# Group-norm statistics moved to ScalarE, and six of eight bases of the last image taken from a neighbour, in a four-layer convolution network

## The chip, the cores and the metric

One NeuronCore of a Trainium2 chip runs the whole batch. The metric is the device time of one launch in microseconds; before the change it is 15807.8 us, the median of three runs from 15794.6 to 15817.1.

A core has TensorE (PE, matmuls into PSUM), VectorE (DVE), ScalarE (ACT, activation functions), GpSimd (POOL, almost unused here) and SyncE (SP), whose queue issues all DMAs. Each engine works through its own instructions in order; semaphores order them across engines.

## The reference, cut to what matters

The input is 8 images of 32 channels, 256 x 256, in fp32. Four layers follow, each `x = x + layer(group_norm(x))`, with 16 groups of two channels:

```python
def _gn(v, G=16, eps=1e-5):          # mean and variance over 2 channels x 256 x 256
    g = v.reshape(B_, G, C_ // G, H_, W_)
    return ((g - mean(g)) / sqrt(var(g) + eps)).reshape(v.shape)

x = x + conv_dynamic(_gn(x))         # layer 0: a 5x5 depthwise filter pooled from the image
x = x + adder(_gn(x))                # layer 1: out[f] = -sum |patch - w[f]| over 32 x 3 x 3, 8 bit
x = x + conv3x3(_gn(x))              # layer 2
x = x + kan_block(_gn(x))            # layer 3
```

Layer 3 has four small KAN networks on 8 x 8 windows. Each normalises its input over 16 or 32 values, takes eight Gaussian bases of every value, and multiplies bases and a SiLU of the input by weights:

```python
GRID = jnp.linspace(-2.0, 2.0, 8); DENOM = 4.0 / 7.0
basis = jnp.exp(-((ln[..., None] - GRID) / DENOM) ** 2)
out = basis.reshape(..., -1) @ ws.T + jax.nn.silu(x) @ wb.T + bb
```

## The kernel before

A chunk is a tile of 128 partitions (four bands of 32 channels) by 2048 fp32 values, eight rows of each band; an image has eight chunks. The layers are the functions `stage0` to `stage3`.

**The planner.** Nothing is issued as it is written down. `Plan.add` records tasks: an engine, an expected time, a rank, the buffers read and written. `Plan.run` then walks through time with these expected times and writes down one order of tasks for all engines: whenever an engine is free it takes the ready task of lowest rank whose buffers fit. That order is what is compiled; on the chip it is fixed. Ranks are in images: layer 1 of image `b` runs beside layers 2 and 3 of image `b-1` and layer 0 of later images. The last image's layers 2 and 3 have no layer 1 beside them; this stretch is called the tail here.

**Buffers.** `ROOM` (line 68) gives places of fixed kinds: three `bas` for bases, three `si`, two `rs`, one `xr`, and a common arena `sb` of ten chunks; `NDV` gives three `dv` slots, used by layer 1 only. In PSUM there is one four-bank place `psB` for layers 0, 2 and 3, one two-bank place `psA` for layer 1 (and for halves of a chunk in the last image's layer 3, `parts`, line 1219), and two one-bank places `psV`.

**Layer 1** is the filler. A pass (`Pass`) makes a quarter of the channels of a quarter of an image: 72 distances `max(q - w, 0)` (line 996 on DVE, whole; line 998 on ACT, in halves, where ACT has been idle), each followed by eight matmuls that add it into `psA` (line 1018). Sixteen passes make an image. PE takes a waiting distance whenever two are queued (`URGENT`), otherwise its other work. At a pass's end ACT evicts `psA` into `xr` (line 1065), the gate of the next pass.

**Statistics.** Every group norm reads its chunks by `add_stats` (line 637): four `bn_stats` of 512 on DVE for a chunk. They follow the eviction that made the chunk, or for layer 0 the load. `finish` (line 647) joins them by `bn_aggr`, averages over partitions by two small matmuls and takes the reciprocal root by hand on DVE. Layer 0 also takes row sums of five overlapping column ranges (`pool`, line 746). Layer 1's input is scaled on ACT (line 967), clipped and rounded by two DVE instructions (972, 973). Layer 2's chunks are normalised on DVE (line 1131).

**Layer 3** goes chunk by chunk (a unit). For each of the four networks: centre by matmul and evict (1234), square (1239), variance by matmul into `psV` (1247), Ln and Exp for the root (1260, 1264), spread by matmul (1279), multiply on DVE (1287). Then `kan`: eight bases, each a Square with bias (1384) and an Exp in place (1397) on ACT. When layer 1 is wholly done, the planner may give the first of the two to DVE instead (`square.other`):

```python
nc.vector.scalar_tensor_tensor(sb(bas), sb(rb), kb2[:, n, k : k + 1], sb(rb), ALU.add, ALU.mult)
```

(line 1390), with the Exp's bias making up for the constant. Eight groups of 16 matmuls in the program (32 in the trace, as fp32) add the bases into `psB` (line 612), then the SiLU part; ACT evicts (1462). The first of the eight waits in the planner until a few bases are done (`HOLD`).

## Time and profile before

| | |
|---|---|
| median of three runs | 15807.8 us |
| profiled execution, its own time | 15810.7 us |
| its span, first to last instruction | 15808.7 us |
| DVE / PE / ACT busy over the span | 85% / 81% / 78% |
| granted TensorE clock, mean | 0.921 |
| first distance on DVE | 435.4 us |
| last distance on DVE | 14485.6 us |

The eight images' layer 1, cut where each image's last `psA` eviction ends, takes 1443, 1942, 1883, 1907, 1737, 1713, 1713 and 1718 us; 1320 us follow. In the first of these stretches no layer 3 runs yet; in the second to fourth, layer 0 of the later images runs beside it; it is all done early in the fifth. A busy PE is not a PE at its peak, since the ends of matmuls are modelled, and a group's mean may hold several shapes.

### The profile page before, as it was taken

The numbers are of one execution on the slowest core, as the hardware profiler recorded it, in microseconds if no ns is written. First come the engines' busy times: TensorE is split into PE (matmuls) and PEld (weight loads), VectorE is DVE, ScalarE is ACT, GpSimd is POOL, SyncE is SP. The second block draws the span as 40 slices with busy tenths as digits, with TensorE's granted clock in tenths as the row PEclk, the third lists the DMA queues.
The fourth block names the chain that finished last, engine by engine and source line by source line (L and its number), as shares of the span: only waits on it lengthen the run. The fifth ranks groups of instructions, "written<-read, shape, count | busy, mean of one in ns | idle before, by whom it ended". The sixth has DMA issues, their size and how long they took to land.

```text
span 15808.7 us, 560681 instructions
## 1 busy us (share of the span) xinstructions
PE 12814.9 (81%) x260296; PEld 4330.4 (27%) x260296; DVE 13427.1 (85%) x12536; ACT 12262.5 (78%) x6849; POOL 33.1 (0%) x25
## 2 busy tenths in 40 slices
PE   6889897887897888888887888778878887887666
PEld 4223232322222222223222222222222222222222
DVE  2898989789878889888899999999999989997465
ACT  0888848678648778676778997799879987997687
POOL 0000000000000000000000000000000000000000
PEclk9989898998998999999999999999999999998777
DMA  4342345446435444554545554454544454444554
GB/s 117 74 101 55 99 118 160 108 123 169 98 97 157 130 118 125 140 139 105 133 123 142 140 131 126 114 140 123 130 127 130 127 128 129 130 132 112 148 154 134
DMA packets 1192870, 1970.85 MB, mean 125 GB/s; under 512 B 362752, under 2 KB 878848, under 8 KB 1092224
## 3 DMA queue, kind: packets, MB, share of 16 engines
q1 hardware_dynamic: 1190528, 1934.98, 46.6%
q8 instruction: 2036, 33.36, 0.9%
q14 instruction: 306, 2.51, 0.1%
HBM read 1162.83 MB, written 771.75 MB: 122 GB/s over the span
## 4 chain that ended last, share of the span: by engine, by line
PE 22%; ACT 20%; DVE 6%; issue 6%; DMA 1%; SPq 0%; DVEq 0%; ACTq 0%
PE psB L612 9%; PE psA L1018 7%; ACT bas L1384 5%; ACT bas L1397 4%; DVE dv L996 3%; ACT arena L1384 2%; PE psB L1148 2%; ACT arena L1397 2%; ACT arena L1234 2%; PE psB L892 1%; ACT si L1462 1%; ACT arena L1239 1%; DVE arena L1287 1%; PE psV L1247 1%; DVE arena L1390 1%
## 5 line engine op out<-in xcount | busy, mean ns | idle before, releaser
L996 DVE TENSOR_SCALAR dv<-qh,w1q 128x4128 bf16<-128x4128 bf16 (+1 forms) x8815 | 10491.2, 1248 | 1358.8 <-PE psA L1018 1289.9
L1018 PE MATMUL psA<-dv,sel_b 128*32 128x512 bf16 x71048 | 5420.4, 403 | 1421.8 <-DVE dv L996 1155.5
L1018 PEld LDWEIGHTS <-sel_b 128*32 128x32 bf16 x82944 | 2047.6, 97 | 6763.7 <-issue 5758.6
L1384 ACT ACTIVATE bas<-arena,kb 128x2048 f32<-128x2048 f32 x1396 | 2782.5, 1993 | 411.8 <-DVE arena L1287 258.6
L1397 ACT ACTIVATE bas<-bas 128x2048 f32<-128x2048 f32 x1396 | 2671.6, 1914 | 40.1
L998 ACT ACTIVATE dv<-qh,w1n 128x2064 bf16<-128x2064 bf16 x832 | 1635.9, 2009 | 1157.6 <-PE psA L1018 1042.0
L612 PE MATMUL psB<-bas,tl 32*32 32x512 f32 x48544 | 1953.2, 653 | 438.8 <-ACT bas L1397 240.1
L892 PE MATMUL psB<-arena,wt 32*32 32x512 f32 (+1 forms) x51040 | 1848.8, 606 | 122.2 <-issue 69.4
L612 PE MATMUL psB<-arena,tl 32*32 32x512 f32 x22368 | 918.8, 619 | 104.0 <-ACT arena L1397 29.0
L612 PEld LDWEIGHTS psB<-bas,tl 32*32 32x32 f32 x48544 | 526.5, 107 | 1327.5 <-ACT bas L1397 514.2
L892 PEld LDWEIGHTS psB<-arena,wt 32*32 32x32 f32 x51040 | 657.5, 104 | 814.0 <-issue 611.4
L1384 ACT ACTIVATE arena<-arena,kb 128x2048 f32<-128x2048 f32 x407 | 810.0, 1990 | 0.0
L1397 ACT ACTIVATE arena<-arena 128x2048 f32<-128x2048 f32 x407 | 779.1, 1914 | 11.6
L643 DVE BATCH_NORM_STATS2 tiny<-arena 128x6 f32<-128x512 f32 x768 | 473.7, 680 | 345.4 <-ACT arena L925 246.4
L1018 PE MATMUL psA<-qh,sel_b 128*32 128x512 bf16 x9216 | 666.3, 394 | 92.1 <-DMA qh<-q 76.8
L1287 DVE TENSOR_TENSOR arena<-psB,arena 128x2048 f32<-128x2048 f32 x280 | 640.0, 2286 | 59.0 <-PE psB L1279 55.9
L1462 ACT ACTIVATE si<-psB,cols_sb 128x2048 f32<-128x2048 f32 x192 | 377.0, 1963 | 385.0 <-PE psB L612 331.5
L612 PE MATMUL psB<-si,tl 32*32 32x512 f32 x14080 | 618.8, 624 | 32.4 <-DVE arena L1287 13.8
L1148 PE MATMUL psB<-arena,tl 32*32 32x510 f32 (+3 forms) x16384 | 626.6, 610 | 19.9 <-issue 19.8
L1239 ACT ACTIVATE arena<-arena 128x2048 f32<-128x2048 f32 x320 | 612.4, 1914 | 9.8
L925 ACT ACTIVATE arena<-psB,cc 128x2048 f32<-128x2048 f32 x64 | 125.6, 1962 | 536.0 <-PE psB L913 536.0
L1234 ACT ACTIVATE arena<-psB 128x2048 f32<-128x2048 f32 x224 | 418.9, 1870 | 127.1 <-PE psB L612 126.5
(151 smaller groups left out, 7406.4 us busy)
## 6 DMA issues: line engine op xcount, KB each, us to landing
arena<-x SPq DMA_DIRECT2D x128, 1024.0 KB
arena<-y SPq DMA_DIRECT2D x128, 1024.0 KB
si<-sy SPq DMA_DIRECT2D x512, 256.0 KB
arena<-in_x_dram SPq DMA_DIRECT2D x240, 384.0 KB
arena<-in_x_dram SPq DMA_DIRECT2D x256, 256.0 KB
x<-arena SPq DMA_DIRECT2D x256, 256.0 KB
xr<-x SPq DMA_DIRECT2D x512, 128.0 KB
x<-xr SPq DMA_DIRECT2D x512, 128.0 KB
```

What stands on the lines that cost most here:

```text
L612: nc.tensor.matmul(view(o[j * C : (j + 1) * C, i - first, :]), w_, src(rows, i, j), start=start, stop=stop)
L892: nc.tensor.matmul(o[:, lo - 2 * j : hi - 2 * j, c0:c1], wt[rows, t, :], d[rows, lo + dy + 2 : hi + dy + 2, c0 + dx : c1 + dx], start=firs ...
L996: nc.vector.tensor_scalar(dst, src, w1q[:, at : at + 1], 0.0, ALU.subtract, ALU.max)
L998: nc.scalar.activation(dst, src, AF.Relu, bias=w1n[:, at : at + 1])
L1018: nc.tensor.matmul(psA[j * C : (j + 1) * C, i, :], sel_b[:, n, :], src[:, at : at + 2, t % 3 : t % 3 + W], **flags,)
L1148: nc.tensor.matmul(o[:, lo - 2 * j : hi - 2 * j, c0:c1], (wc if t == 4 else tl[:, W2T + t, :])[rows], d[rows, lo + dy + 1 : hi + dy + 1, c ...
L1234: lambda ps=ps, at=at: nc.scalar.activation(sb(c)[:, at], ps().rearrange("p s f -> p (s f)"), func, bias=shift),
L1239: plan.add("ACT", 1.9, lambda: nc.scalar.activation(sb(sq), sb(c), AF.Square), r=[c], w=[sq], rank=rk)
L1287: lambda ps=ps, at=at: nc.vector.tensor_tensor(sb(c)[:, at], ps().rearrange("p s f -> p (s f)"), sb(c)[:, at], ALU.mult),
L1384: lambda k=k, bas=bas: nc.scalar.activation(sb(bas), sb(rb), AF.Square, bias=kb[:, n, k : k + 1]),
L1397: lambda k=k, bas=bas, square=square: nc.scalar.activation(sb(bas), sb(bas), AF.Exp, scale=-1.0, bias=0.0 if square.eng == "ACT" else kbsq ...
L1462: nc.scalar.activation(sb(o), psB.rearrange("p s f -> p (s f)"), AF.Identity, bias=obias)
```

## The change

1. **Statistics.** Sums come from the accumulator output of the evictions that made the chunks (layer 0: from the row sums, less the columns counted twice). Squares come from a Square on ACT with an accumulator, shifted by the first chunk's mean (`add_squares`), in place of `bn_stats`. The squares themselves go to a scratch half behind the chunk, so that chunks and `xr` are longer.
2. **Layer 2's normalisation** goes from DVE to ACT.
3. **The clip** of layer 1's input comes after the rounding, on bf16.
4. **Last image, layer 3.** Of eight bases, numbers 2 and 5 are made by Square and Exp, both on ACT. The other six are a neighbour times `exp(2v)` or `exp(-2v)` times a constant, one `scalar_tensor_tensor` on DVE each; the two ratios are two Exp on ACT of a clamped input (one DVE instruction).
5. **Choice of engine.** When layer 1 is wholly done, the planner may also give the evictions and squares of the variances to DVE (`evict.other`, `square.other`). The product of line 1390 stays for images before the last.
6. **Buffers.** In the same stretch bases and `si` may take the `dv` slots. `BASE_SPARE` goes from three chunks to two, `HOLD` from 4 to 3. In the last image two `si` loads of the third network may start after the first base, not the fifth. A rule on PE's order (`AHEAD`) goes.

```diff
-ROOM = [("bas", 3 * BASE, BASE), ("si", 3 * F, F), ("rs", F // 2, F // 4), ("xr", F // 2, F // 2), ("sb", 10 * F, 0)]
-AHEAD = 9.0
+CHAIN = ((2, None), (5, None), (3, 2), (1, 2), (4, 5), (6, 5), (0, 1), (7, 6))
+MID, FAR = 3, 20.0
+ROOM = [("bas", 3 * BASE, BASE), ("si", 3 * F, F), ("rs", F // 2, F // 4), ("xr", 3 * F // 4, 3 * F // 4), ("sb", 10 * F, 0)]
-BASE_SPARE = 3 * F
-HOLD = 4
+BASE_SPARE = 2 * F
+HOLD = 3
...
             if b.base:
-                b.kind = "bas" if self.places["bas"] else "sb"
+                b.kind = "bas" if self.places["bas"] else "dv" if self.over() and self.places["dv"] else "sb"
                 spare = BASE_SPARE
+            if b.side:
+                b.kind = "si" if self.places["si"] or not self.over() else "dv" if self.places["dv"] else "sb"
...
-                        if best is not None and e == "PE" and best.rank > self.image() + AHEAD:
-                            piece = self.fill(e, False)
-                            if piece is not None:
-                                best = piece
...
+    def over(self):
+        return all(p.done for p in self.passes[self.first_pass :])
...
+        def add_squares(self, src, at, i, size, rank):
+            if not self.chunks & 1 << i:
+                self.chunks |= 1 << i
+                plan.add(
+                    "DVE", 0.16,
+                    lambda: nc.vector.tensor_scalar(
+                        self.shift[:, i : i + 1], self.sums[:, at : at + 1], -1.0 / size, None, ALU.mult
+                    ),
+                    r=[src, self.summed], w=[self.shifted[i]], rank=rank,
+                )
+            plan.add(
+                "ACT", 0.25 + 0.85e-3 * size,
+                lambda: nc.scalar.activation(
+                    sb(src)[:, size : size + size // 2].bitcast(BF16), sb(src, size), AF.Square, bias=self.shift[:, i : i + 1],
+                    accum_out=self.squares[:, at : at + 1],
+                ),
+                r=[src, self.shifted[i]], w=[self.bufs[at]], rank=rank,
+            )
...
+                total, both = norm.sums[:, k : k + 1], norm.d[:, 0, 0:1]
+                nc.vector.tensor_reduce(total, rowsum[:, :, k * R : (k + 1) * R], AX.XY, ALU.add)
+                nc.vector.tensor_reduce(both, v[:, :, 51:205:51], AX.XY, ALU.add)
+                nc.vector.tensor_tensor(total, total, both, ALU.subtract)
-            norm.add_stats(xt, 4 * k, [], r(0.02 * k))
-            plan.add("DVE", 2.9, pool, r=[xt], w=[rs_buf[k]], rank=r(0.02 * k))
+            plan.add("DVE", 3.4, pool, r=[xt], w=[rs_buf[k], norm.summed], rank=r(0.02 * k))
+            norm.add_squares(xt, k, 0, F, r(0.02 * k))
...
-            norm1.add_stats(xt, 4 * k, [], rk)
+            norm1.add_squares(xt, k, 0, F, rk)
...
-                    nc.vector.tensor_scalar(sb(t, F), sb(t, F), QMAX, -QMAX, ALU.min, ALU.max)
                     nc.vector.tensor_scalar(q16(t), sb(t, F), ROUND, ROUND, ALU.add, ALU.subtract)
+                    nc.vector.tensor_scalar(q16(t), q16(t), QMAX, -QMAX, ALU.min, ALU.max)
...
-                norm.add_stats(xr, 8 * g + 2 * h, [], rk, 2)
+                norm.add_squares(xr, NH * g + h, g, F // 2, rk)
...
-                nc.vector.tensor_scalar(sb(xt), sb(xt), norm.mean, norm.rs, ALU.subtract, ALU.mult)
-            plan.add("DVE", 1.7, normal, r=[norm.done], w=[xt], rank=rk)
+                nc.scalar.activation(sb(xt, 10 * W), sb(xt, 10 * W), AF.Identity, bias=nmr, scale=norm.rs)
+            plan.add("ACT", 2.4, normal, r=[sm["c2"]], w=[xt], rank=rk)
...
-            norm3.add_stats(xo, 4 * k, [], rk)
+            norm3.add_squares(xo, k, 0, F, rk)
...
+                evict.other = "DVE", 0.15 + 2.1 * us, lambda ps=ps, at=at: nc.vector.tensor_scalar(
+                    sb(c)[:, at], ps().rearrange("p s f -> p (s f)"), shift, None, ALU.add
+                )
...
+            square.other = "DVE", 2.3, lambda: nc.vector.tensor_tensor(sb(sq), sb(c), sb(c), ALU.mult)
...
+            if last:
+                up, down = Buf("sb", F), Buf("sb", F)
+                plan.add(
+                    "DVE", 1.3,
+                    lambda: nc.vector.tensor_scalar(sb(up), sb(rb), kmax[:, n : n + 1], kmin[:, n : n + 1], ALU.min, ALU.max),
+                    r=[rb], w=[up], rank=rk, spare=SPARE,
+                )
+                for o, sign, bias in ((down, -2.0, kdn[:, n : n + 1]), (up, 2.0, kb2[:, n, MID : MID + 1])):
+                    plan.add(
+                        "ACT", 1.9,
+                        lambda o=o, sign=sign, bias=bias: nc.scalar.activation(
+                            sb(o), sb(up), AF.Exp, scale=sign, bias=bias
+                        ),
+                        r=[up], w=[o], rank=rk, table=LN_EXP, spare=SPARE,
+                    )
+            for k, k0 in chain:
+                bas = bases[k]
+                if k0 is not None:
+                    ratio = up if k > k0 else down
+                    by = float(np.exp(2 * (MID - k0) * (k - k0) - 1))
+                    exps.append(plan.add(
+                        "DVE", 2.4,
+                        lambda bas=bas, k0=k0, ratio=ratio, by=by: nc.vector.scalar_tensor_tensor(
+                            sb(bas), sb(bases[k0]), by, sb(ratio), ALU.mult, ALU.mult
+                        ),
+                        r=[bases[k0], ratio], w=[bas], rank=rk,
+                    ))
+                    continue
...
-                square.other = "DVE", 2.45, product
+                square.other = None if last else ("DVE", 2.45, product)
```

The evictions of layers 0, 1 and 2 also gain `accum_out=` a column of `sums`. The ranks of layer 3's parts are written out by the caller (`beside`) and, but for the SiLU of `z`, are the same numbers.

## The prediction

> **What bounds the kernel now.** I read the page's shares and slices first, then the busy time of stretches cut where an image's sixteenth `psA` eviction (L1065) ends, then the waits inside them, then groups by form. The page:
>
> ```profile
> PE 12814.9 (81%) x260296; PEld 4330.4 (27%) x260296; DVE 13427.1 (85%) x12536; ACT 12262.5 (78%) x6849; POOL 33.1 (0%) x25
> ...
> PEclk9989898998998999999999999999999999998777
> ```
>
> No engine is saturated, and the last slices are another regime. By stretch (an image with a chunk of layer 0 beside it, one without, then the two parts of the tail):
>
> ```profile
> 3818.00:5701.00 1883.00, 1601.41 (x33804) 513.97 (x33800) 1627.29 (x1549) 1320.41 (x730) 6.21 (x2) 0.94 0.47 122
> ...
> 11058.00:12771.00 1713.00, 1393.02 (x26884) 448.70 (x26884) 1583.16 (x1343) 1486.22 (x836) 3.90 (x2) 0.94 0.49 129
> ...
> 14489.00:14710.00 221.00, 146.94 (x3412) 75.03 (x3412) 87.34 (x119) 81.87 (x46) 0.00 (x0) 0.79 0.53 136
> 14710.00:15809.00 1099.00, 718.91 (x12840) 235.97 (x12832) 634.99 (x323) 860.53 (x532) 0.00 (x0) 0.74 0.53 146
> ```
>
> Columns: length, then busy PE, PEld, DVE, ACT, POOL, clock, DMA share, GB/s. Without layer 0, DVE is busy 1583 of 1713 us (92%), ACT 87%. With it, PE rises to 85%, DVE falls to 86% and ACT to 70%. The tail, last image alone, has ACT at 78%, PE at 65%. Waits of the layer-0 stretch:
>
> ```profile
> PE psA L1018 <- DVE dv L996: 105.5, 182, 5.0
> ...
> DVE dv L996 <- PE psA L1018: 223.3, 235, 20.4
> ```
>
> There DVE waits on PE twice as long as PE on DVE. In 11058 to 12771 it is the reverse: PE on DVE 190, DVE on PE 114. So the main part is bound by both, coupled through three `dv` slots. The rows that price the change:
>
> ```profile
> L643 DVE BATCH_NORM_STATS2 tiny<-arena 128x6 f32<-128x512 f32 x768 | 473.7, 680 | 345.4 <-ACT arena L925 246.4 <-ACT arena L1164 73.1 <-DMA arena<-in_x_dram 21.5
> ...
> L1390 DVE SCALAR_TENSOR_TENSOR arena<-arena,kb 128x2048 f32<-128x2048 f32 x124 | 285.5, 2346 | 4.2 <-PE psV L1247 3.3 <-issue 0.9
> ...
> L967 ACT ACTIVATE arena<-arena,cc 128x2048 f32<-128x2048 f32 x64 | 132.8, 2087 | 28.8 <-DMA arena<-x 28.8
> ...
> L1131 DVE TENSOR_SCALAR arena<-arena,tiny 128x2560 f32<-128x2560 f32 x64 | 102.8, 1608 | 25.1 <-DMA arena<-x 25.1
> ```
>
> **What the Trainium skill says.** "ScalarE: Activation LUTs", What ACT_TABLE_LOAD costs: any function costs 0.833 ns per element, 280 ns fixed with a pointer bias, 93 ns more per pointer. That gives 1990 at 2048 (L1384: 1993) and 2.5 us for the new 2560-wide normalisation (L967, two pointers: 2087 at 2048). "VectorE: DVE Perf Modes", the perf-mode tier table: fp32 tensor_scalar 1227 ns at 2048 (L973: 1227), bf16 693. The same page, Two Vector instructions with no wait between them, calls an accumulator output two instructions; whether ScalarE's is, and its time, no row here shows.
>
> **The change, in the trace's sum.** Profiled execution: span 15808.7, its own time 15810.7, median 15807.8; these are one number. Counts by image come from the order of the built programs, durations from the rows, counted start to start where an engine runs back to back (four bn_stats take 2.39 us, a distance 1.23, an L1390 2.29).
>
> *DVE in the main part.* 1024 bn_stats go; 84 of them stand before DVE's first distance and 34 in the tail, so 906 x 0.60 = 544 us. Normalisation moves to ACT: 56 x 1.55 = 87. The clip runs on bf16: 56 x 0.55 = 31. Added: three small sums per layer-0 chunk (some 0.45 us, about 25), and 83 full distances that ACT did in halves (83 x 1.23 less 27 halves of 0.70 = 83). Statistics' small operations cancel against bn_aggr. Fourteen scalings (2.25) and some other stage-3 work go to the tail, about 36. With what moves across the boundaries the orders give, image by image, 1308, 1679, 1629, 1652, 1619, 1587, 1600, 1585 before (within 2% of the measured busy times) and 1204, 1592, 1568, 1533, 1560, 1552, 1559, 1537 after: 12659 to 12105, 554 less.
>
> *ACT in the main part.* Added: 168 squares of 2048 (1.95) and 127 of 1024 (1.1), 468 us; 56 normalisations of 2.5, 140. Accumulator reads, some 560: nothing at the low end, 0.28 us (one short pointer instruction) at the high; I take 0.2, 112. Gone: 139 distance halves x 2.0, 278; and the stage-3 work of the last image but one that the new order leaves for the tail: 95 bases (3.9 us a pair), 12 evictions and their squares, some 450. Sum: about level (11285 to 11255), by image 1250, 1375, 1401, 1360, 1429, 1409, 1558, 1473. ACT has room except in image 6 (1558 against 1486).
>
> *PE.* No matmul is dropped. Three units of stage 3 (about 55 us each at 1.08 per block of 32) leave the main part, and layer 0 spreads: 8 chunks an image to image 5, where the old order had 11 to 14 in images 1 to 3. At 0.49 us per gather and 1.06 to 1.10 per block, images 0 to 7 go from 1144, 1473, 1445, 1460, 1270, 1244, 1245, 1250 to 1068, 1369, 1361, 1349, 1385, 1377, 1255, 1255.
>
> *What that is worth.* The eight stretches of before (1443 to 1942 us) are fitted within 12 us by 0.74 PE + 0.68 DVE - 292, and images 1 to 7 within 9 by 0.80 PE + 0.45 DVE. The weights say what a microsecond off DVE buys while the engines wait on one another. On the new work they give 460 and 340 off the main part. ACT at its best share so far (0.877) would hold image 6 near 1776 us where they want 1700, so I take 370.
>
> *Start-up.* The first eight chunks are paced by DVE (bn_stats 2.4 + pooling 2.45). With statistics on ACT the DMA sets it: 10 saved. The layer-0 taps that follow are PE's; nothing else moves.
>
> *Tail.* It now begins with 117 bases of the last image but one (22 before): 3.7 units of stage 3 mixed with layer 2. Up to the last layer-2 eviction ACT goes from 80 to 396 us of work, DVE from 88 to 313, PE from 113 to 286. At 0.80 on ACT that is 495 us instead of 221: 274 more. Behind it, eight units of the last image alone. A group of eight bases cost up to eight products (2.3) on DVE and eight exponentials on ACT; now two squares, two ratios and two exponentials on ACT (6 x 1.95) and one clamp and six products on DVE (1.25 + 13.8). With 45 halves of evictions and 20 squares moved to DVE: ACT 849 to 603, DVE 637 to 694, PE unchanged. ACT was 77% busy over 1099 us. If DVE takes that share, 694/0.77 = 900: 200 less. Each product waits for its neighbour's exponential and for both ratios; behind it on DVE stand the next group's scalings, and behind those PE's broadcasts, which already wait 92 us there for L1287. Six bas and dv places instead of three (dv lies idle in the tail), and lower HOLD and spare, I cost at nothing: they let the bases run ahead of the single `psB`, which is what makes the 77% possible; without that cover PE would wait as it does now for L1397 (51.6 + 27.9), some 80 us. Net of the tail: 75 longer.
>
> Queues: SP issues 6280 DMAs in both, and each xt or xr is now released by a square instead of bn_stats; the residual load behind it has most of a 107 us pass to arrive. The shift that a square waits for is one tiny DVE instruction, once per group. Evictions now have a square behind them on ACT, about 2 us before the next exponential: paid above.
>
> Sum: -10 - 370 + 75 = -305, so **15500 us**, 1.9% less.
>
> **Rivals.** *DVE is the bound throughout.* For: 92% in images 5 to 7. Main shrinks by 554/0.894 = 620 and the tail stays level, since three engines now share it: 15180. Against: DVE's waits on PE with layer 0.
> *PE is the bound.* For: the waits of 3818 to 5701, and matmul work is untouched. Only 117 of PE work leaves the main part: 117/0.83 = 140 less, tail 75 more, start 10 less: 15730.
> *The debt comes due in the tail (slower).* The mechanism is the backlog of 117 bases, run where there is no distance work to fill gaps. If its part goes at 0.65 on ACT (610) and the units behind at 0.66 on DVE (1050), as coupled groups on one `psB` and a clock of 0.74 would have it, the tail grows by 340; with PE bounding the main part (150 less) the kernel ends at 16000. It decides once the tail outgrows what is saved ahead of it: beyond 1700 us (now 1320) against the forecast's 380, beyond 1480 against 160.
>
> **How the numbers follow.** A measurement tells 0.2% (30 us) from nothing. Forecast 0.58, DVE-bound 0.18, PE-bound 0.14, debt 0.10. The forecast's own range, fit of 340 to 460 and tail of -20 to +160, is 15320 to 15620. Reaching to the two faster cases' middles: 15200 to 15740, leaving the debt and the ends. Faster: everything but the debt and a sliver of the PE case, 0.87; same 0.04; slower 0.09.
>
> **What would show it.** Right: last distance ends at 14080 to 14150; images 1 to 5 even at 1760 to 1820, 6 and 7 at 1680 to 1780; DVE's share in the main part still 88 to 91%; no bn_stats rows; squares at 1.95 to 2.0; the tail near 1400, layer 2 ending near 500 into it, then units of 105 to 120 us. Wrong: ACT above 90% in images 4 to 7 (accumulators dearer than 0.3 us), or PE's waits on DVE gone while DVE's on PE grow (PE-bound), or units at 130 us again.

## The result and the profile after

The changed kernel takes 15624.0 us (median of four, 15616.6 to 15634.7) against 15808.5 for the kernel before in the same comparison: a ratio of 0.9885, 95% interval 0.9868 to 0.9902. The forecast was 15500. The profiled execution has a span of 15620.1, 188.6 less than before. Cut as the prediction cut it, that is 8 from the start-up, 533 from the eight stretches of the main part (1231, 1800, 1790, 1734, 1784, 1763, 1750, 1671 us for images 0 to 7), and 353 back in the tail.

The page of the changed kernel, the two rows shown of before:

```profile
PE 12724.2 (81%) x260296; PEld 4307.3 (28%) x260296; DVE 13070.3 (84%) x12057; ACT 12264.1 (79%) x7416; POOL 21.2 (0%) x25
...
PEclk9989999999999999999999999999999999987677
```

The shares hardly moved. DVE lost 357 us in all, ACT gained 2, and the low clock of the tail now covers the last four slices where it covered three. The busy time of stretches, cut at the same events (length, then busy PE, PEld, DVE, ACT, POOL, clock, DMA share, GB/s): image 2 with layer 0 beside it, image 7 without, and the two parts of the tail.

```profile
3456.00:5246.00 1790.00, 1502.66 (x30906) 484.65 (x30898) 1554.85 (x1476) 1396.30 (x852) 2.69 (x2) 0.95 0.49 128
...
12277.00:13948.00 1671.00, 1365.74 (x26116) 433.80 (x26108) 1526.68 (x1281) 1473.11 (x878) 1.37 (x1) 0.94 0.48 129
13948.00:14530.00 582.00, 360.90 (x8094) 162.98 (x8094) 301.09 (x166) 400.18 (x240) 0.00 (x0) 0.74 0.53 137
14530.00:15621.00 1091.00, 701.85 (x12870) 263.23 (x12870) 695.26 (x417) 606.43 (x379) 0.00 (x0) 0.72 0.55 149
```

The main part ends at 13948 instead of 14489. The first part of the tail (last layer-1 eviction to last layer-2 eviction) grows from 221 to 582 us. The second (the eight units of the last image) takes 1091 where it took 1099, although ACT has 254 us less to do in it. The waits of the layer-0 stretch, on PE and then on DVE (us in total, how many, the longest):

```profile
PE psA L1073 <- DVE dv L1051: 134.0, 239, 2.8
...
DVE dv L1051 <- PE psA L1073: 210.1, 218, 31.7
```

Before, over 1883 us, they were 105.5 and 223.3. DVE still waits longer on PE than PE on DVE, but the gap is narrower. The rows by form that answer to the priced ones (count, then busy us and mean ns of one; bn_stats is gone):

```profile
L675 ACT ACTIVATE arena<-arena,tiny 128x2048 bf16<-128x2048 f32 x192 | 383.6, 1998 | 67.8 <-DMA arena<-in_x_dram 42.0 <-DVE tiny L668 23.0
L1467 DVE SCALAR_TENSOR_TENSOR bas<-bas,arena 128x2048 f32<-128x2048 f32 x81 | 185.0, 2290 | 80.2 <-ACT bas L1488 44.9 <-PE psB L623 34.7
L1188 ACT ACTIVATE arena<-arena,cc,tiny 128x2560 f32<-128x2560 f32 x64 | 159.8, 2511 | 0.0
...
L1028 DVE TENSOR_SCALAR arena<-arena 128x2048 bf16<-128x2048 bf16 x64 | 44.4, 694 | 2.2
L1448 DVE TENSOR_SCALAR arena<-arena,kmax,kmin 128x2048 f32<-128x2048 f32 x32 | 43.1, 1347 | 1.3
...
L675 ACT ACTIVATION_READ_ACCUMULATOR arena<-arena,tiny 128x1 f32 x192 | 36.0, 187 | 0.0
```

The large prices of the prediction hold: squares 2.0 us, the normalisation 2.51 (2.5), a product 2.29 (2.3), the bf16 clip 0.69. Two small ones were too low: the clamp (L1448) took 1.35 for 1.25, and the three small sums of a layer-0 chunk (L799 to L801) took 0.55 together for 0.45. The accumulator, for which no row of before existed, is a separate instruction of 187 ns (0.2 was taken).

### The profile page after: what moved, and what is told of

Same layout as the page of the kernel before. It is cut to its first block, busy times and chain, and to the rows that moved or that the text cites. A ratio compares the mean times of both kernels' runs of the same rounds, so it can differ in the third digit from the quotient of the medians.

```text
span 15620.1 us, 560335 instructions
## 1 busy us (share of the span) xinstructions
PE 12724.2 (81%) x260296; PEld 4307.3 (28%) x260296; DVE 13070.3 (84%) x12057; ACT 12264.1 (79%) x7416; POOL 21.2 (0%) x25
## 5 line engine op out<-in xcount | busy, mean ns | idle before, releaser
L1073 PE MATMUL psA<-dv,sel_b 128*32 128x512 bf16 x70800 | 5341.6, 400 | 1233.8 <-DVE dv L1051 1030.6
L623 PE MATMUL psB<-bas,tl 32*32 32x512 f32 x49184 | 1990.7, 651 | 516.3 <-ACT bas L1488 247.6
L1053 ACT ACTIVATE dv<-qh,w1n 128x2064 bf16<-128x2064 bf16 x668 | 1319.2, 2011 | 1058.6 <-PE psA L1073 1026.9
L623 PEld LDWEIGHTS psB<-bas,tl 32*32 32x32 f32 x49184 | 544.8, 107 | 1410.9 <-issue 541.4
L945 PEld LDWEIGHTS psB<-arena,wt 32*32 32x32 f32 x51040 | 615.3, 104 | 788.0 <-issue 630.0
L1352 DVE TENSOR_TENSOR arena<-psB,arena 128x2048 f32<-128x2048 f32 x280 | 640.6, 2288 | 217.5 <-PE psB L1344 212.8
L623 PE MATMUL psB<-arena,tl 32*32 32x512 f32 x17696 | 696.3, 617 | 133.7 <-ACT si L1553 43.3
L1475 ACT ACTIVATE arena<-arena,kb 128x2048 f32<-128x2048 f32 x353 | 702.6, 1990 | 0.2
L1488 ACT ACTIVATE arena<-arena 128x2048 f32<-128x2048 f32 x353 | 675.7, 1914 | 10.2
L1205 PE MATMUL psB<-arena,tl 32*32 32x512 f32 (+3 forms) x16384 | 634.6, 613 | 30.4 <-issue 30.4
L623 PE MATMUL psB<-si,tl 32*32 32x512 f32 x14048 | 621.7, 621 | 43.5 <-ACT si L1553 17.8
L1303 ACT ACTIVATE arena<-arena 128x2048 f32<-128x2048 f32 x290 | 555.2, 1914 | 8.8
L1344 PE MATMUL psB<-rs,tl 32*32 32x512 f32 x8960 | 351.6, 652 | 211.6 <-DVE arena L1352 109.3
```

What stands on the lines that cost most here:

```text
L623: nc.tensor.matmul(view(o[j * C : (j + 1) * C, i - first, :]), w_, src(rows, i, j), start=start, stop=stop)
L945: nc.tensor.matmul(o[:, lo - 2 * j : hi - 2 * j, c0:c1], wt[rows, t, :], d[rows, lo + dy + 2 : hi + dy + 2, c0 + dx : c1 + dx], start=firs ...
L1053: nc.scalar.activation(dst, src, AF.Relu, bias=w1n[:, at : at + 1])
L1073: nc.tensor.matmul(psA[j * C : (j + 1) * C, i, :], sel_b[:, n, :], src[:, at : at + 2, t % 3 : t % 3 + W], **flags,)
L1205: nc.tensor.matmul(o[:, lo - 2 * j : hi - 2 * j, c0:c1], (wc if t == 4 else tl[:, W2T + t, :])[rows], d[rows, lo + dy + 1 : hi + dy + 1, c ...
L1303: square = plan.add("ACT", 1.9, lambda: nc.scalar.activation(sb(sq), sb(c), AF.Square), r=[c], w=[sq], rank=rk)
```

## The experiments

All runs in one table: median, ratio to the kernel before on the same chip with its 95% interval, end of the main part, and the two parts of the tail. A runs to the last layer-2 eviction. B runs from there to the last layer-3 eviction; the last store to DRAM, some 6 us, is left out here, so B is 1092 before and 1085 after. Then the busy times of PE, DVE and ACT in B, in us, and the granted clock there.

| run | median | ratio (interval) | main ends | A | B | PE, DVE, ACT in B | clock in B |
|---|---|---|---|---|---|---|---|
| before | 15807.8 | 1 | 14489 | 221 | 1092 | 719, 635, 861 | 0.74 |
| after | 15624.0 | 0.9885 (0.9868 to 0.9902) | 13948 | 582 | 1085 | 702, 695, 606 | 0.72 |
| e1 statistics alone | 15690.3 | 0.9930 (0.9913 to 0.9946) | 13824 | 726 | 1134 | 729, 656, 885 | 0.74 |
| e2 last image alone | 15754.6 | 0.9970 (0.9959 to 0.9982) | 14477 | 177 | 1091 | 708, 698, 604 | 0.71 |
| e3 no neighbour's bases | 15621.1 | 0.9882 (0.9867 to 0.9896) | 13941 | 584 | 1085 | 700, 738, 780 | 0.75 |
| e4 backlog early | 15658.3 | 0.9908 (0.9893 to 0.9923) | 14264 | 294 | 1088 | 705, 696, 607 | 0.71 |
| e5 psA in quarters | 15908.8 | 1.0065 (1.0050 to 1.0080) | 13944 | 582 | 1373 | 911, 712, 608 | 0.67 |
| e6 few products | 15595.2 | 0.9867 (0.9851 to 0.9883) | 13926 | 580 | 1076 | 697, 303, 606 | 0.72 |
| e7 few matmuls | 15655.3 | 0.9906 (0.9891 to 0.9921) | 13935 | 577 | 1135 | 766, 696, 609 | 0.60 |
| e8 fewer bytes | 15609.5 | 0.9872 (0.9858 to 0.9887) | 13961 | 578 | 1067 | 696, 695, 606 | 0.72 |
| e9 whole psB | 15645.2 | 0.9898 (0.9883 to 0.9913) | 13930 | 584 | 1104 | 622, 689, 604 | 0.70 |
| e10 added matmuls | 15756.7 | 0.9965 (0.9952 to 0.9978) | 13945 | 584 | 1223 | 881, 707, 598 | 0.77 |
| e11 e3 without lending | 15653.3 | 0.9902 (0.9882 to 0.9922) | 13816 | 713 | 1122 | 713, 755, 803 | 0.74 |
| e12 links cut | 15521.1 | 0.9820 (0.9803 to 0.9838) | 13922 | 587 | 994 | 704, 689, 606 | 0.75 |

Two questions are asked: which part of the change earns what, and why B stays near 1090 us whatever is taken off an engine. The first theory for B was that the succession of a unit's steps paces it (the chain theory); the rivals were ACT's, DVE's and PE's work, and the transfers. The expectations call the first rival, with the forecast's pricing, the work theory.

### Which part earns what (e1, e2, e3, e11)

e1, from the changed kernel, leaves only the statistics, the normalisation and the clip; the new name of `other` keeps evictions and squares of the last image on ACT, and the two early `si` loads wait for the fifth base again. (The rule `AHEAD` stays out in every run here, so what it was worth isn't shown.)

```diff
-BASE_SPARE = 2 * F
-HOLD = 3
+BASE_SPARE = 3 * F
+HOLD = 4
...
-                b.kind = "bas" if self.places["bas"] else "dv" if self.over() and self.places["dv"] else "sb"
+                b.kind = "bas" if self.places["bas"] else "sb"
...
-            chain = CHAIN if last else [(k, None) for k in range(GRID)]
+            chain = [(k, None) for k in range(GRID)]
...
-                evict.other = "DVE", 0.15 + 2.1 * us, lambda ps=ps, at=at: nc.vector.tensor_scalar(
+                evict_other = "DVE", 0.15 + 2.1 * us, lambda ps=ps, at=at: nc.vector.tensor_scalar(
...
-            square.other = "DVE", 2.3, lambda: nc.vector.tensor_tensor(sb(sq), sb(c), sb(c), ALU.mult)
+            square_other = "DVE", 2.3, lambda: nc.vector.tensor_tensor(sb(sq), sb(c), sb(c), ALU.mult)
```

> The statistics alone: squares and sums on ScalarE, normalisation on ScalarE, the bf16 clip; the last image keeps the form of before (eight squares or products and eight Exps in a group, no buffers lent, no evictions or squares moved to VectorE). Chain theory (the units of the last image are paced by the succession of their steps through one psB, not by any engine's work): the main part ends near 13950 as in the changed kernel, the tail stays within 60 of its 1672, total 15590 to 15690. Work theory (ScalarE's work paces the tail, as the forecast's pricing has it): the tail's ScalarE work goes from 1009 back towards 1260 to 1420 with the backlog still in it, at 78% busy 1620 to 1820 us of tail, total 15690 to 15830.

Measured: 15690.3. The chain theory missed the main part, and both theories missed the tail: the main part ends 665 us earlier than before, 124 earlier than in the changed kernel, and the tail takes 1860, with A at 726. More of the last-but-one image's layer 3 is left over for it. The total sits at the common edge of the two expectations and decides nothing between them.

e2 is the complement: `add_squares` is `add_stats` again in all four places, accumulators gone, normalisation on DVE and the fp32 clip:

```diff
-            norm1.add_squares(xt, k, 0, F, rk)
+            norm1.add_stats(xt, 4 * k, [], rk)
...
-                nc.scalar.activation(sb(xt, 10 * W), sb(xt, 10 * W), AF.Identity, bias=nmr, scale=norm.rs)
+                nc.vector.tensor_scalar(sb(xt, 10 * W), sb(xt, 10 * W), norm.mean, norm.rs, ALU.subtract, ALU.mult)
```

> The last image's part alone: bases from a neighbour, lent buffers, work of the last image that may move to VectorE; statistics (bn_stats), normalisation and clip stay on VectorE as before. Chain theory: the main part ends within 50 of 14489 and the tail within 60 of 1320, total 15730 to 15850. Forecast's pricing (units at the pace of 77% of the busiest engine): units of the last image 900 instead of 1099, total near 15610.

Measured: 15754.6, as the chain theory had it. With no new backlog in the way, B is 1091 against 1092, with ACT's work in it down from 861 to 604 us. The profiled execution is 57 us shorter than that of before: 12 at the main part's end and 44 in A.

e3 takes out the neighbour's bases alone:

```diff
-            chain = CHAIN if last else [(k, None) for k in range(GRID)]
+            chain = CHAIN if False else [(k, None) for k in range(GRID)]
...
-            if last:
+            if False:
                 up, down = Buf("sb", F), Buf("sb", F)
...
-                square.other = None if last else ("DVE", 2.45, product)
+                square.other = "DVE", 2.45, product
```

> The changed kernel, but the last image's bases are all made from their own square (or product) and Exp, as in the images before it; the rest of the change stays. Chain theory: total within 60 of 15624, units of the last image still 130 to 145 us each. Work theory: ScalarE and VectorE take back some 150 and 110 us of work in the tail, which grows by 120 to 200, total 15740 to 15830.

Measured: 15621.1, the time of the changed kernel. B in the busy times of stretches:

```profile
14525.00:15610.00 1085.00, 700.00 (x12870) 243.57 (x12870) 737.78 (x429) 779.91 (x462) 0.00 (x0) 0.75 0.54 149
```

ACT has 173 us more work and DVE 43 more than with the neighbour's bases, and B has the same 1085 us. The neighbour's bases, the most elaborate part of the change, earn nothing here.

e11 takes the lending out of e3; evictions and squares may still move:

```diff
-BASE_SPARE = 2 * F
-HOLD = 3
+BASE_SPARE = 3 * F
+HOLD = 4
...
-                b.kind = "bas" if self.places["bas"] else "dv" if self.over() and self.places["dv"] else "sb"
+                b.kind = "bas" if self.places["bas"] else "sb"
-            if b.side:
-                b.kind = "si" if self.places["si"] or not self.over() else "dv" if self.places["dv"] else "sb"
```

> The changed kernel without the bases from a neighbour (which moved nothing) and without the lent places: dv isn't lent to bases or side inputs, HOLD 4 and BASE_SPARE as before; evictions and squares of the last image may still move to VectorE. The statistics alone gave 15690 and the change without the bases from a neighbour 15621. If the lent places make the 70 between them: total 15670 to 15700. If the work that may move to VectorE does: 15610 to 15640.

Measured: 15653.3, between the two expectations. From e1 to e11 (work that may move to DVE) the ratio falls from 0.9930 to 0.9902, and from e11 to e3 (lending) to 0.9882. Each step is about 30 to 45 us, and the intervals of neighbouring runs overlap, so the split between these two stays open; the first step also holds the two early `si` loads, which e11 keeps and e1 doesn't. That both together earn some 70 us is clear of the intervals.

### Is the backlog a debt? (e4)

A rule is added to the planner's step for PE, so that PE works off what lies behind:

```diff
-                    best = self.fill(e, True)
+                    best = None if e == "PE" and self.behind(ready[e]) else self.fill(e, True)
...
+    def behind(self, ready):
+        p = next((p for p in self.passes[self.first_pass :] if not p.done), None)
+        if p is None or not LAG:
+            return False
+        at = p.b + (4 * p.h + p.g) / 16 - LAG
+        return any(t.rank < at and not (t.gate and not t.gate(self)) and self.fits(t.need, t.spare) for t in ready)
```

> The changed kernel with one rule added to the planner: TensorE takes a ready piece of another stage ahead of a distance when that piece lies 0.4 of an image or more behind the distances, so that the backlog of bases is worked off inside the main part. Theory that the backlog is only moved (its work costs the same wherever it stands): the last distance ends 200 to 300 later than 13948, the tail is as much shorter (near 1400), total within 60 of 15624. Theory that the backlog is a debt (dear in the tail, where no distances fill the gaps): the main part grows by 100 to 150 only and the tail falls by 250 to 300, total 15430 to 15530.

Measured: 15658.3. Image 6 and the two parts of the tail:

```profile
10728.00:12561.00 1833.00, 1458.20 (x28044) 484.95 (x28028) 1538.42 (x1290) 1640.07 (x969) 2.69 (x2) 0.93 0.48 126
...
14264.00:14558.00 294.00, 186.84 (x4524) 99.65 (x4518) 107.95 (x80) 178.51 (x112) 0.00 (x0) 0.78 0.53 132
14558.00:15646.00 1088.00, 704.92 (x12870) 261.39 (x12870) 695.61 (x417) 606.80 (x379) 0.00 (x0) 0.71 0.54 148
```

A falls by 288 us and the main part ends 316 later. What moved is no debt: the same work costs about as much in either place. And B, entered with far less left over, is 1088.

### What paces the last image's units (e5 to e10)

Each of these takes work, or adds it, on one resource in the last image.

e5 gives `psA` to centring and spreading in four quarters of one bank:

```diff
-            return [(Buf("psA"), lambda: psA, i, 0.5) for i in (0, 2)]
+            four = [Buf("qA") for _ in range(4)]
+            return [(p, lambda p=p: psA[:, p.at : p.at + 1], i, 0.25) for i, p in enumerate(four)]
```

> The changed kernel, but in the last image the results that go through psA (centring and spreading matmuls) use its two banks as two places of 512 columns in turn, where the changed kernel has one place of two banks and TensorE and VectorE alternate on it (2.04 us of spreading, 1.24 us of scaling, twice over, one after the other: 6.6 us a pair; in quarters 4 x 1.02 + 0.7 = 4.8). If this single place is a link of the chain that paces the last image, some 80 pairs in the tail by 1.8 us, half or more of them on the chain: tail 60 to 130 shorter, total 15490 to 15565. If it lies beside other waits: total within 30 of 15624, or up to 40 longer for the more numerous small instructions.

Measured: 15908.8, a miss on both sides. The chain of work of this kernel (start, duration, what, and how many records) shows two reasons at once:

```profile
15017.81 1.97 PE psA L623 x8
...
15019.81 0.70 DVE arena L1301
...
15020.55 1.97 PE psA L1345 x8
...
15022.55 0.70 DVE arena L1301
```

The two engines still alternate: PE starts a quarter when a read by DVE ends, and DVE's next read starts when that quarter is done, though it reads an older one. The eviction L1301 at 15022.55 reads a centring (L623) and starts when the spreading L1345 ends. In all of B, DVE's L1353, which reads spreadings, waits 68.5 us behind L623, and L1301 waits 33.1 us behind L1345. In this edit the two banks are one tile (`psA`); whether that causes it isn't shown, and so two places that really take turns stay untested. And a quarter with half the matmuls of a half (8 records for 16) takes PE as long: 1.97 us against the 2.04 below. Twice the handoffs, each at full price, cost 288 us of B.

e6 makes the products on 64 of 2048 columns, and lets PE read a constant for the rest:

```diff
-                            sb(bas), sb(bases[k0]), by, sb(ratio), ALU.mult, ALU.mult
+                            sb(bas)[:, :64], sb(bases[k0])[:, :64], by, sb(ratio)[:, :64], ALU.mult, ALU.mult
```

> Part of the computation is left out, same order of instructions: in the last image the six products of each group on VectorE are made on 64 of their 2048 columns, and TensorE takes a constant for the columns that are missing. VectorE loses some 190 x 2.2 = 420 of its 695 us behind layer 2. If VectorE's work sets the pace there, the tail falls by 250 or more (total under 15370). Chain theory: only the waits on products in the chain go (VectorE's products hold about 80 to 100 us of it), tail 40 to 120 shorter, total 15500 to 15585.

```profile
14506.00:15582.00 1076.00, 697.38 (x12870) 270.02 (x12870) 303.05 (x417) 606.18 (x377) 0.00 (x0) 0.72 0.55 150
```

Measured: 15595.2. DVE's work in B falls from 695 to 303 us, and B by 9. DVE's work isn't the pace; the chain theory expected 40 or more, so the products' own links are cheaper than it had them.

e7 leaves one matmul of sixteen for the bases made by a product:

```diff
-                    lambda bas=bases[k]: mm16(psB, tl[:, WK + 9 * n + k, :], spans(sb(bas)), first, False, view=view),
+                    lambda bas=bases[k], k=k: (one if last and k not in (2, 5) else mm16)(
+                        psB, tl[:, WK + 9 * n + k, :], spans(sb(bas)), first, False, view=view
+                    ),
```

> Part of the computation is left out, same order of instructions: in the last image TensorE does one of the sixteen matmuls for each of the six bases made by a product; ScalarE's and VectorE's work stays. TensorE loses some 190 x 1.7 = 325 of its 702 us behind layer 2. If TensorE's work sets the pace, the tail falls by 250 or more (total under 15370). If the chain runs through TensorE about half of the time, by 100 to 170 (15455 to 15525). If TensorE only waits for the bases that ScalarE and VectorE make, by less than 60.

The stretch, then the group of single matmuls, then the whole groups of the changed kernel:

```profile
14512.00:15647.00 1135.00, 766.14 (x7110) 170.33 (x7110) 695.52 (x417) 608.69 (x379) 0.00 (x0) 0.60 0.52 141
```

```profile
L627 PE MATMUL psB<-bas,tl 32*32 32x512 f32 x232 | 161.7, 799 | 13.0 <-DVE bas L1473 12.9
```

```profile
L623 PE MATMUL psB<-bas,tl 32*32 32x512 f32 x5504 | 292.7, 734 | 108.9 <-ACT bas L1488 88.0 <-ACT si L1553 9.5 <-DVE bas L1467 5.9
```

Measured: 15655.3, outside every expectation, because the premise was false. 116 single matmuls (two records each) are 161.7 us, 1.39 each; a whole group of sixteen takes 1.70 in the changed kernel (292.7 us for 172 groups of 32 records). The records of a group overlap, for 5504 of them with a mean of 734 ns lie in 292.7 us. So the other fifteen matmuls of a group add about 0.31 us together (at clocks of 0.60 and 0.72), and there was little to take away. PE's busy time rises from 702 to 766 us, with a granted clock of 0.60 instead of 0.72, and B is 50 us longer. This run can't say whether less PE work would shorten B; in it, B got longer as PE's steps did.

e8 halves the bytes of ten transfers per unit (`y`, `yd`, the SiLUs, `oa`, `od`, `sz` to DRAM, and the loads of `y` and `yd`):

```diff
+        def move(dst, src):
+            n = dst.shape[1] // 2 if last else dst.shape[1]
+            nc.sync.dma_start(dst[:, :n], src[:, :n])
...
-lambda d=d, a=a: nc.sync.dma_start(d, sb(a))
+lambda d=d, a=a: move(d, sb(a))
```

> Part of the data is left out, same order of instructions: in the last image's layer 3 the stores of y, yd, their Silu, oa, od and sz to DRAM and the loads of y and yd move half of their bytes (about 5 of 20 MB per unit). If the transfers set the pace of the units (146 GB/s were moved there at a mean DMA share of 0.55), the tail falls by 100 or more (total under 15525). If not, total within 40 of 15624.

Measured: 15609.5. B is 1067, 18 less for a quarter of the bytes (149 GB/s in the changed kernel, 112 now, in the stretch). The bytes are not the pace. The number of transfers is the same, so what a transfer takes beside its bytes isn't tested.

e9 sends centring and spreading through `psB` in one piece, as in the images before:

```diff
-            if not last:
+            if True:
                 return [(Buf("psB"), lambda: psB, 0, 1.0)]
```

> The changed kernel, but in the last image centring and spreading go through psB in one piece of 2048 columns, as in the images before it, instead of through psA in two halves. In the traces so far a psA half (8 matmuls, half of the array's row groups) takes TensorE 0.94 to 1.1 us at full clock and 2.04 us at the lower one, and so does a quarter with 4 matmuls, while a whole group of 16 takes 1.2: the split doubles TensorE's time for them. Theory that TensorE's own time paces the last image (behind layer 2 the units took 1.49 to 1.56 times TensorE's busy time in nine kernels, whatever VectorE and ScalarE did): 80 second halves of 1.1 to 1.8 us go, TensorE's 702 us there fall to 560 to 610, the units take 870 to 950 instead of 1085, total 15400 to 15490. Rival: psB now holds the four bases groups of a unit and all its centring and spreading one after the other, and the waits for it eat the gain: tail level or longer by 50 to 200, total 15620 to 15820.

The spreading matmuls behind layer 2, first in the changed kernel, in halves, then here, whole:

```profile
L1344 PE MATMUL psA<-rs,tl 32*32 32x512 f32 x1280 | 141.6, 873 | 76.5 <-DVE arena L1352 56.9 <-ACT rs L1329 19.6
```

```profile
L1344 PE MATMUL psB<-rs,tl 32*32 32x512 f32 x1280 | 71.1, 925 | 80.3 <-ACT rs L1329 30.6 <-DVE arena L1352 22.8 <-ACT si L1553 16.7
```

The premise held: 80 halves at 1.77 us become 40 wholes at 1.78, and PE's busy time in B falls from 702 to 622. But B is 1104. The waits of PE behind layer 2 in e9:

```profile
PE psB L623 <- ACT bas L1488: 114.2, 22, 10.3
PE psB L623 <- DVE arena L1352: 94.9, 18, 11.3
```

In the changed kernel the first is 88.0, and `psB` doesn't wait for L1352 at all behind layer 2, since the halves go through `psA`. The rival came true: the one `psB` takes back what PE gains. And the rule of thumb that B is some 1.5 times PE's busy time, which nine kernels had followed, fails here: 1104 is 1.77 times 622.

e10 adds zero-weight matmuls while an accumulation is open, to keep the granted clock up:

```diff
+                    if best is None and e == "PE" and self.open and self.over():
+                        best = self.filler("PE", 0.55, self.idler, [], [], lambda t: None)
```

> The changed kernel with work added: in the tail, where the planner sees TensorE idle while an accumulation in psB is open, TensorE does eight matmuls of zero weights that add nothing to it. If the low granted clock (0.72 behind layer 2, 0.95 in the main part) is part of what makes TensorE slow there: clock 0.85 or more in the tail, the same groups of matmuls 10 to 15% shorter, tail 60 to 120 shorter, total 15500 to 15565. If the clock is not the point, or the added matmuls stand ahead of work that has become ready: total 15620 to 15720.

```profile
L613 PE MATMUL psB<-tl,nought 32*32 32x512 f32 x3824 | 264.1, 595 | 5.6 <-issue 5.6
L1361 PE MATMUL psA<-rs,tl 32*32 32x512 f32 x1280 | 143.6, 879 | 74.4 <-DVE arena L1369 39.2 <-ACT rs L1346 26.9 <-DVE arena L1317 8.3
```

Measured: 15756.7, worse by 133 and outside both expectations. 264 us of added matmuls lifted the clock of B from 0.72 to 0.77, and the spreading matmuls, where PE waits for a short link each time, were no faster (879 ns against 873). Whether a clock kept high would help isn't answered; this way doesn't keep it high where it matters.

### Cutting links and nothing else (e12)

What all these left alone is the order of steps. A piece of the chain of work of the changed kernel, within a unit:

```profile
14993.73 1.98 PE psV L1312 x8
...
14995.74 0.70 ACT rs L1325
...
14996.45 0.64 ACT rs L1329
...
14997.14 2.04 PE psA L1344 x16
...
14999.27 1.24 DVE arena L1352
...
15000.55 2.04 PE psA L1344 x16
...
15002.61 1.24 DVE arena L1352
...
15007.22 1.36 DVE arena L1448
...
15009.12 1.99 ACT arena L1454
15011.14 2.00 ACT arena L1454
15013.14 1.80 ACT bas L1488
```

Variance, two roots, spreading and scaling in turn, the clamp: each step waits for the one before it, and the work passes between PE, ACT and DVE. From the two ratios (L1454) on, the chain follows ACT's own order. In these 21 us (14993.7 to 15014.9) PE is busy for 9.8, DVE for 7.6 and ACT, which has other work too, for 17.0. PE's waits behind layer 2 in the changed kernel are such links:

```profile
PE psB L623 <- ACT bas L1488: 88.0, 22, 9.1
...
PE psV L1312 <- DVE arena L1304: 48.9, 18, 3.8
...
PE psV L1312 <- ACT arena L1303: 20.3, 13, 3.2
PE psA L1344 <- ACT rs L1329: 19.6, 13, 2.0
```

e12 keeps every instruction and cuts these: `some` is a constant in SBUF, and `fixed` gives slices of it. Of each line only the operands are shown:

```diff
-tl[:, VAR + n, :], sb(sq)[:, s * FS : (s + 1) * FS],
+tl[:, VAR + n, :], some if last else sb(sq)[:, s * FS : (s + 1) * FS],
-tl[rows, BC + 4 * n + g, :], sb(rs, FS)[rows],
+tl[rows, BC + 4 * n + g, :], some[rows] if last else sb(rs, FS)[rows],
-psB, tl[:, WK + 9 * n + k, :], spans(sb(bas)), first, False, view=view
+psB, tl[:, WK + 9 * n + k, :], fixed if last else spans(sb(bas)), first, False, view=view
```

> Part of the computation is left out, but no instruction: in the last image's layer 3 TensorE's matmuls for the variance, for spreading and for the bases read a constant instead of the squares, the roots and the bases. Every engine has the same instructions in the same order; only TensorE's waits on the squares (49 + 20 us behind layer 2 in the changed kernel), on the roots (20) and on the exponentials and products (88 + 6) are cut, 183 us of the 383 that it is idle there. Theory that the steps' succession paces the last image: units behind layer 2 shorter by 100 or more (1085 to 985 or less), total under 15530. Theory that the instructions themselves, two-bank psA and one psB pace it (the waits move to the next handoff): less than 50 shorter, total 15570 to 15630.

```profile
14509.00:15503.00 994.00, 704.18 (x12870) 282.24 (x12870) 689.17 (x415) 606.44 (x377) 0.00 (x0) 0.75 0.59 162
```

```profile
PE psA L623 <- ACT arena L1300: 66.9, 9, 11.0
```

Measured: 15521.1, 103 less than the changed kernel and under the chain theory's 15530; B is 994, 9 above its 985. The busy times of all three engines in B are those of the changed kernel to within 7 us, and B is 91 us shorter, so the 91 us come from waits alone. 183 us of PE's waits were cut, and PE's idle time in B fell from 383 to 290, so half came back as other waits. The largest is PE's wait for ACT's eviction of `psA` (line 1300 here, 1295 in the changed kernel), 66.9 us where 4.6 stood.

One more wait went with them, which the expectation doesn't name. A product that is written over an old base has to wait until PE has read that base, and here PE reads no base. DVE's wait for it in B of the changed kernel, which has no counterpart in e12:

```profile
DVE bas L1467 <- PE psB L623: 40.2, 35, 3.4
```

So e12 shows that waits between engines set part of B's pace: 91 us, about a quarter of PE's idle time there. It doesn't separate waits for data from waits for a free buffer, and how the other 290 us divide among `psA`, `psB` and ACT's order isn't shown.

## Why the prediction was right and where it was wrong

**Sign and range: right, and in part by luck.** 15624 lies in 15200 to 15740, and the two movements of the forecast, a faster main part that pays some of it back in the tail, are what happened. But neither has the size that was given to it. Saved in the main part: 541 with the start-up (380 predicted, 470 at most); given back: 353 (75 predicted, 160 at most). The two errors of 161 and 278 us went against each other, so the miss of 124 is smaller than either. The forecast's own range, 15320 to 15620, just misses the result; the wider range holds it because it reaches towards the rivals.

**The signs.** DVE's share of the main part (89%), the missing bn_stats rows and squares of 2.0 us are as named. The main part ended earlier than named (the last distance started at 13941, for an end at 14080 to 14150), and the tail took 1673 us for some 1400. One sign of being wrong came true: units at 130 us again (1091 us for eight, 136 each).

**Start-up:** 8 for 10.

**Work in the main part.** DVE fell by 580 (554 by image; the prediction's items alone add up to 590), ACT by 105 (30). PE was mis-sized: its busy time fell from 11707.8 to 11421.5 us, by 286, where counting by image gave 112, although the three units named there are 165. Images 1 to 3 lost 356 where 299 was counted, images 4 to 7 gained 189 for 263, and image 0 lost 120 for 76.

**What that is worth.** The first fit gave 460 for the eight stretches; measured 533. It gave 1316, 1802, 1780, 1748, 1792, 1781, 1696, 1681 and was within 1% on six of eight; image 6 is 3% off (1750) and image 0 7% (1231). Image 6 is the stretch that ACT was to hold: ACT is 89% busy in it, and 1776 was named. But the step from 460 to 370 took 90 for it, and 54 was right. Image 0, with no layers 2 and 3 beside it, gave 212 for the 127 of the fit: its waits of ACT on `psB`, 89.6 us, fell to 8.2, and DVE's on `psA` from 116.2 to 33.2. Of the 163 missed in the stretches, 90 were taken off the fit by choice and 85 are image 0's; the other stretches cancel to 12.

The second fit, which described the kernel before as closely (within 9 us), gave 340, and nothing known then told the two apart. Their inputs were counts. Fitted again to the busy times in the trace of before, the first form is 0.74 PE + 0.54 DVE - 178 and the second, for images 1 to 7 alone, 0.78 PE + 0.39 DVE. With the busy times of the changed kernel the first gives 526 for the eight stretches (533 measured) and the second 314 for images 1 to 7 (321 measured). So with measured work each comes near on the stretches that it was fitted to, though in the first image 0 stays 5% off and image 6 3%.

**The tail's first part.** The work of ACT and DVE was right (ACT 400 for 396, DVE 301 for 313); PE's grew by 214 for 173. The 0.80 on ACT was not right: 0.69, and 582 us for 495. That is nearer the debt rival's 0.65 and 610. But e4 shows that it is no debt: 288 us less here cost 316 in the main part.

**The tail's second part: the step that failed.** "If DVE takes that share, 694/0.77 = 900." DVE's work was 695, ACT's 606 (603 predicted), and the units took 1091. A share of the busiest engine is no property that another engine inherits when work is moved. e2 takes 256 us from ACT with the statistics of before, e3 gives ACT 173 us back, e6 takes 392 from DVE, e9 takes 80 from PE, and B stays between 1076 and 1104; e12 takes no work at all, only waits, and B is 994. The 77% was not ACT's limit in the first place. The same holds for the lent places, costed at nothing because they made the 77% possible: with the work that may move to DVE they earn some 70 us (e1 against e3). 49 of these only undo a loss: statistics alone had lengthened B from 1092 to 1134, and e3 brings it to 1085, about the level of before.

**The rivals.** *DVE-bound* (15180) had 620 off the main part, nearer to the measured 533 than the forecast's 370. Against it stand images 4 to 6: DVE's work in them fell by 62, 32 and 44 us, and they took 47, 50 and 37 us longer. And the tail, level by its account, took 353 us longer. *PE-bound* (15730) had 140 off the main part; even the measured 286 us of PE's work, divided by its own 0.83, are 345. So neither engine alone sets the main part. *The debt* had the tail right (A 610, B 1050, for 582 and 1091) and the total wrong: it saw only 150 saved ahead, and 541 were. It was to decide once the tail outgrows what is saved ahead of it; with 541 saved that is beyond 1861 us, and the tail took 1673.

## What to carry to other kernels

Where engines wait on one another in a steady stretch, a fit of its length to the busy times of several engines can predict a change, within 1% on six of eight stretches here. But two fits that described the old kernel equally well differed by 120 us on the new one, so keep both, as a range. In a stretch with little independent work, like B, busy shares didn't tell what removing work is worth: look for the chain of steps first, and test it by cutting a link while every instruction stays. A cut link also frees the buffers that it held, so look at both. And when a faster main part leaves work over for the end, look for whether that work is merely moved: here it cost about the same in both places.

The bases from a neighbour could be left out: the kernel without them (e3) takes the same time with a simpler last image. No version run here is clearly faster than the changed kernel with the whole computation.

## What the hardware showed that was not expected

PE's time for a group of 32 x 32 matmuls grows much less than their number. One took 1.39 us (e7, clock 0.60), four (a quarter of a spread) 1.71 (e5, 233.1 us for 136 groups, clock 0.67), eight 1.77 (the changed kernel, 0.72), sixteen 1.78 (e9, 0.70). The Trainium skill has the mechanism ("TensorE: Matmul & The Clock Gate", Packing small matmuls — row/col tiling): matmuls at different tile positions run at once in the array. The traces agree, and add what it means for a split: a chunk cut into halves by row groups costs PE twice, 141.6 us instead of 71.1. Halves cut by columns weren't tried.

The same page (What's actually happening) says that the array's clock is gated by how busy PE has been. The tail agrees only in part. With fifteen of sixteen matmuls gone for three quarters of the last image's bases the clock fell from 0.72 to 0.60 (e7), but PE's busy share of B rose there from 65% to 67%, so the clock didn't follow the busy share that the trace shows. And 264 us of added matmuls lifted it only to 0.77 (e10).

An accumulator output on ACT is an instruction of its own, 187 to 194 ns, 576 of them in the kernel.
